# A graph network whose instruction order a planner writes: bias rows by an eight-column matmul, more raw weight buffers on two queues, and TensorE's clock in the planner's estimate

## The chip, the cores and the metric

One Trainium2 chip, one core of it. The metric is the device time of one execution in microseconds. The kernel before took 3004.77 us, the median of three runs (3003.74, 3004.77 and 3006.28).

## The reference

Thirty-two independent graphs of 512 nodes with 128 features go through four layers. Each layer takes a layer norm and a ReLU of x, runs its graph network on the result, and adds that to x.

```
# layer 0: maximum over neighbours
p = x @ (W1 - W2); q = x @ W2
out[i] = max over j of relu(p[i] + q[j] + b) * adj[i, j]

# layer 1: four steps, tanh, with earlier outputs stacked in front of later steps
src_agg = l2norm(adj, rows) @ (nodes @ ws + bs)
dst_agg = l2norm(adj, columns).T @ (nodes @ wd + bd)
self_rep = nodes @ wn + bn
out = tanh(concat(src_agg, self_rep, dst_agg) @ wu + bu)

# layer 2: mean over neighbours
out = (adj / rowsum) @ (x @ weight) + bias

# layer 3: four steps of a GRU
m = adj.T @ (h @ weight[i]); gx = m @ w_ih.T + b_ih; gh = h @ w_hh.T + b_hh
r = sigmoid(xr + hr); z = sigmoid(xz + hz); n = tanh(xn + r * hn)
h = (1 - z) * n + z * h
```

Everything is fp32. The adjacency matrix holds zeros and ones, about one in 32 of them ones.

## The kernel before

**One order for everything.** A batch is one graph. The Python functions `prepare`, `gathers`, `layer1` and `layer23` do not issue instructions. They note operations on a `Flow` object, each with its engine, an assumed duration, the operations it depends on and a due time. `Flow.run` then plays a little model of the five engines: `step` picks, among the operations whose inputs are ready and whose buffers are free, the one that can begin first (among equals the one that is due first), issues it, and moves the model's time on. The kernel's instructions stand on each engine in the order in which `step` issued them, and the engine works them off in that order. All of them are issued by one line in `step`, so that every row of the profile names line 496; tiles tell the operations apart.

**Due times and leads.** The due time of an operation is its part's place times `PACE`, less the assumed length of the work behind it in its part, less a lead. Each stage of a batch has its lead in `LEADS` (line 40). Place n is the batch's number, shifted for the last four by `LAST`. The weights are two parts ahead of the batches, `first` and `rest`, with the places in `WEIGHTS`. At most `AHEAD` = 6 parts are open at a time. Operations of some five batches are therefore mixed on each engine.

```python
PACE = 45.29
AHEAD = 6
WEIGHTS = (-4.52, -3.22)
```

**A batch.**
- `prepare`: norm of x; transposes of the adjacency matrix (tiles `pat`, then `at`); `pq`, the products with W; counts of neighbours as a matmul with a triangle of ones (`pc`, copied to `cc`, and by small DMAs on SP to `ccd`); keys of the neighbours that the counting leaves (`pkey`, whose eight largest DVE takes as `top`, and `idx` from it). `qn` goes to a table in DRAM, `qtab`.
- `gathers`: the first four neighbours in each group of rows by one-hot matrices `oh` that DVE makes and PE multiplies with `qhl` (`pa`), with a running maximum `acc` on DVE; up to seven further neighbours by 28 indirect DMAs on POOL from `qtab` (`gm`, `G`), with maxima on DVE. At the end `px`, `x1`, and four loads `an` of the adjacency matrix.
- `layer1`: `xn` is split into a high and a low part (`hi`, `lo`) so that two fp32r products with `at` and `an` (`pg`) give the aggregation in nearly fp32. The four steps multiply the results with folded weights `w1` in fp32 (`pu`), with the bias rows `b8` as a first product, with `rows`. After tanh the feature `f` is transposed again (`pf`) for the next step.
- `layer23`: layer 2 (`pg2`, `mT2`, `po`), then four GRU steps (`pk` for two gates, `pg3` for the messages, `mT`, `phn`, `pxn`). A step ends with a chain on two engines, from `pxn` over DVE, tanh on ACT and two more DVE operations to the new state, which PE transposes (`ph`) and ACT and DVE split into `hi` and `lo` for the next step. The output is stored by ACT's queue.

**Buffers.** PSUM has 8 banks, kept by `BANKS` = (2, 1, 2, 1) for four stages, with two more for whoever needs one. Scratch tiles are rings with one to six slots; weights borrow the rings that the batches use later.

**The weights.** `FastWeights.rest` (line 646) loads 16 bias rows and two blocks of GRU biases into `brow`, one DMA each on SP, and transposes them (`pb`, `bcol`). For each of the four steps of layer 1 it loads `wu` and, one after the other through one ring "f", `ws`, `wn` and `wd`; each is transposed (`pwt`), copied by DVE (`wt`), multiplied with `wu` (`pw`) and copied by ACT (`w1`). The two bias rows of a step are products with one column (`pv`); DVE splits them into a high and a low half (`both`), and eight one-row DMAs on SP for each step spread them over the eight rows of `b8`. Then come the weights of layers 2 and 3: `graw_hh` and `graw_ih` of the four GRU steps go through one ring, "gate1", all on SP, and are transposed (`pg_hh`, `pg_ih`).

Of the kernel before, what the change touches and what calls it, by code (L numbers as in the profile page):

```python
# [13 lines left out]
F32 = mybir.dt.float32  # L14
# [10 lines left out]
P = 128  # L25
# [6 lines left out]
KEY = float(ROWS)  # L32
CODES = ((0, 1), (P, 1), (2 * P, 2), (4 * P, 4))
NLEFT = 7
PACE = 45.29
SPACING = 1.8
AHEAD = 6
BANKS = (2, 1, 2, 1)

LEADS = {  # L40
    "prepare": -31.3, "counts": -26.1, "keys": -29.9, "rows": -0.7,
    "gather0": 21.0, "gather1": 4.8, "gather2": 6.6, "gather3": -2.6,
    "first": 14.3, "layer1": -15.8, "layer10": -31.7, "layer11": -34.7,
    "layer12": -17.6, "layer13": -49.5, "layer2": 17.3, "layer3": 7.8,
    "layer30": 58.6, "layer31": 78.0, "layer32": 33.2, "layer33": 37.4,
    "out": 22.6,
}
LAST = (0.0, 0.0, 0.06, -0.57, -0.08)
WEIGHTS = (-4.52, -3.22)
LN_EPS = 1e-5  # L50
L2_EPS = 1e-12
LOWEST = float(np.finfo(np.float32).min)
# [226 lines left out]
class Flow:  # L279
# [6 lines left out]

    LAT = 0.06
    LOAD = 0.25
    EVENT = 0.13
    ENGINES = ("pe", "vec", "act", "pool", "sync")  # L290

    def __init__(self, nc, pace, ahead, slack=0.0):
        self.nc, self.pace, self.ahead, self.slack = nc, pace, ahead, slack
        self.rings, self.part, self.lanes = {}, [], {}
        self.lead = 0.0
        self.free = dict.fromkeys(self.ENGINES, 0.0)
        self.busy = dict.fromkeys(self.ENGINES, 0.0)
        self.gathered, self.port, self.turn, self.queue = 0.0, 0.0, 0, {}
        self.seen = {e: {} for e in self.ENGINES}
        self.waiting = {e: [] for e in self.ENGINES}  # L300
        self.vec = Engine(self, "vec", nc.vector)
        self.act = Engine(self, "act", nc.scalar)
        self.pool = Engine(self, "pool", nc.gpsimd)
        self.sync = Engine(self, "sync", nc.sync)
# [22 lines left out]
    def cost(self, engine, op, outs, ins):  # L327

        aps = outs + ins
        n = max(a.free_size() for a in aps)  # L330
        o = outs[0].free_size()
        if "dma" in op:
            if engine != "pool":
                width = 2 if outs[0].dtype == BF16 else 4
                return 0.4, 2.0 + outs[0].size() * width / 1.5e5
            return (1.25, 6.0) if "indirect" in op else (0.7, 4.0)
        if engine == "vec":
            if op == "tensor_scalar" and o > 256:
                t = o / 1920.0 + 0.157
            elif op == "bn_stats":  # L340
                t = 0.28
            else:
                t = (o if op != "max" else n) / 960.0 + 0.15
                if op == "scalar_tensor_tensor" and len(ins) == 3:
                    t += 0.06
            return t - 0.082 + (0.08 if len(outs) > 1 else 0.0), 0.082
        if engine == "act":
            t = o / 1200.0 + 0.16 + 0.1 * (len(ins) - 1) + (0.04 if in_sbuf(ins[0]) else 0.0)
            return t - 0.1 + (0.2 if len(outs) > 1 else 0.0), 0.1
        if op == "tensor_tensor" and o < 64:  # L350
            return 1.1 if o < 8 else 1.7, 0.0
        two = op in ("tensor_tensor", "tensor_add", "tensor_sub", "tensor_mul")
        return (o / 408.0 + 0.05 if two and o > 64 else o / 1100.0 + 0.18), 0.0
# [99 lines left out]
    def step(self):  # L453
# [20 lines left out]
        seen.update(need)  # L474
        self.turn += 1
        op.turn = self.turn
        cost = op.cost + (self.EVENT * max(0, len(need) - 1) if op.engine != "pe" else 0.0)
        op.end = self.free[op.engine] = t + cost
        if op.port:
            self.port = op.end  # L480
# [23 lines left out]
                self.enter(u)  # L504
        self.log(op, t)
        return op

    def log(self, op, t):
        pass
# [55 lines left out]
class FastWeights:  # L565
# [5 lines left out]
    def __init__(self, nc, F, a, const, mid, ps):  # L571
# [37 lines left out]
        for t in range(n // P):  # L609
            nc.vector.tensor_scalar(  # L610
                self.code[:, t, :], ident, code[:, t : t + 1], None, ALU.mult
            )
        self.nc, self.a, self.const, self.n = nc, a, const, n

    def own(self, shape, dtype, name):
# [30 lines left out]
    def rest(self):  # L646
# [13 lines left out]
        col, at = {}, 0  # L660
        for key, src, m in rows:
            col[key] = at
            F.sync.dma_start(out=brow[at : at + m, :], in_=src)
            at += m
        pb = self.psum("pb")
        F.tr(pb[:, 0, :], brow, ident)
# [7 lines left out]


        self.w1, self.bu = [], self.own([P, NL1], F32, "bu")
        b8 = self.temp("hg", "b8")
        for i in range(NL1):
            ch = NCH[i]
            wu = self.temp("x2", f"wu{i}")[:, 0:3, :]  # L680
            F.sync.dma_start(out=wu, in_=a[f"L1_gnn_wu{i}"].rearrange("(c p) v -> p c v", p=P))
            w1 = self.own([P, 3, ch, P], F32, f"w1_{i}")
            for k, nm in enumerate(("ws", "wn", "wd")):
                w = self.temp("f", f"{nm}{i}")[:, 0:ch, :]
                F.sync.dma_start(
                    out=w, in_=a[f"L1_gnn_{nm}{i}"].rearrange("(c p) v -> p c v", p=P)
                )
                pt = self.psum(f"pwt_{i}_{k}")
                for c in range(ch):
                    F.tr(pt[:, c, :], w[:, c, :], ident)  # L690
                wt = self.temp("gate0", f"wt_{i}_{k}")[:, 0:ch, :]
                F.vec.tensor_copy(wt, pt[:, 0:ch, :])
                pw = self.psum(f"pw_{i}_{k}")
                for c in range(ch):
                    F.mm(pw[:, c, :], wt[:, c, :], wu[:, k, :], start=True, stop=True)
                F.act.copy(w1[:, k, :, :], pw[:, 0:ch, :])
            self.w1.append(w1)
            pv = self.psum(f"pv_{i}")
            c = col["bn", i]
            F.mm(pv[:, 2, 0:1], wu[:, 1, :], bcol[:, c : c + 1], start=True, stop=True)  # L700
            for k, nm in enumerate(("bs", "bd")):
                c = col[nm, i]
                F.mm(pv[0:1, k, :], bcol[:, c : c + 1], wu[:, 2 * k, :], start=True, stop=True)
            c = col["bu", i]
            F.vec.tensor_add(self.bu[:, i : i + 1], bcol[:, c : c + 1], pv[:, 2, 0:1])
            both = self.temp("agf1", f"both_{i}", True)
            part = both[0:1, 0, 0:256].bitcast(F32R)
            F.vec.tensor_copy(part, pv[0:1, 0:2, :].rearrange("p k d -> p (k d)"))
            F.vec.tensor_sub(
                both[0:1, 1, 0:256], pv[0:1, 0:2, :].rearrange("p k d -> p (k d)"),  # L710
                both[0:1, 0, 0:256],
            )
            for h in range(2):
                for g in range(2):
                    for k in range(2):
                        r = 4 * h + 2 * g + k
                        F.sync.dma_start(
                            out=b8[r : r + 1, i, :], in_=both[0:1, h, k * P : (k + 1) * P]
                        )
        self.b8 = self.own([8, NL1, P], F32R, "b8r")  # L720
        F.vec.tensor_copy(self.b8, b8[0:8, :, :])

        self.w2 = self.own([P, P], F32, "w2")
        F.sync.dma_start(out=self.w2, in_=a["L2_gnn_weight"])
        self.b2 = self.own([P, P], F32, "b2")
# [10 lines left out]
        self.gh, self.gm = [], []  # L736
        for l in range(NL3):
            for nm, dst in (("hh", self.gh), ("ih", self.gm)):
                g = self.temp("gate1", f"graw_{nm}{l}")[:, 0:3, :]
                F.sync.dma_start(  # L740
                    out=g, in_=a[f"L3_gnn_w_{nm}"][l].rearrange("(g p) c -> p g c", p=P)
                )
                pg = self.psum(f"pg_{nm}{l}")
                for k in range(3):
                    F.tr(pg[:, k, :], g[:, k, :], ident)
                t = self.own([P, 3, P], F32, f"g_{nm}{l}")
                if nm == "hh":
                    F.vec.tensor_copy(t, pg[:, 0:3, :])
                else:
                    gt = self.temp("xn2", f"gt_{l}")[:, 0:3, :]  # L750
                    F.vec.tensor_copy(gt, pg[:, 0:3, :])
                    pf = self.psum(f"pf_{l}")
                    F.mm(
                        pf[:, 0:3, :].rearrange("p t d -> p (t d)"), w3t[:, l, :],
                        gt.rearrange("p t d -> p (t d)"), start=True, stop=True,
                    )
                    F.act.copy(t, pf[:, 0:3, :])
                dst.append(t)
# [12 lines left out]
def fast(ctx: ExitStack, tc: tile.TileContext, a: dict, out: bass.AP, bad):  # L771
# [9 lines left out]
    dram = ctx.enter_context(tc.tile_pool(name="table", bufs=1, space=DRAM))  # L781

    F = Flow(nc, PACE, AHEAD)
    F.share(ps, 8, {f"ps{s}": n for s, n in enumerate(BANKS)})

    def bank(s, shape, dtype, name):
        return F.tile(ps, shape, dtype, f"ps{s}", name, BANKS[s])
# [388 lines left out]
    def batch(b):  # L1176
# [8 lines left out]

    places = [b - LAST[max(0, b - B + len(LAST) - 1)] for b in range(B)]
    F.run(
        [(WEIGHTS[0], W.first), (WEIGHTS[1], W.rest)]
        + [(p, partial(batch, b)) for b, p in enumerate(places)]
    )  # L1190

# [469 lines left out]
```

## Time and profile before

| what | value |
|---|---|
| median of three runs | 3004.77 us (3003.74 to 3006.28) |
| profiled execution | 3005.68 us, span 3004.0 us |
| PE busy | 2821.0 us, 94% of the span |
| DVE busy | 2403.8 us, 80% |
| POOL busy | 1798.9 us, 60% |
| ACT busy | 1214.9 us, 40% |
| granted TensorE clock | 0.979 of full speed, mean |
| chain that ended last | PE 77%, DVE 12%, issue 4%, ACT 2%, DMA 1%, POOL 1% |

The profile is one execution. PE is TensorE's products, PEld its weight loads, DVE VectorE, ACT ScalarE, POOL GpSimd, SP SyncE; a q behind a name is that engine's DMA queue. The row of slices gives busy tenths in 40 equal slices of the span, 75.1 us each, and PEclk the clock that TensorE was granted, in tenths. An f32 matmul stands as two records. A list of waits gives, for each engine and tile, for whom it waited: us in total, times, longest. The chain that ended last follows the work back from the last instruction. In what follows "the list" of an engine is the order of its instructions in the built program.

### The profile page before, as it was taken

Reading aid. Unit: us, or ns where it says so; the run is one execution under the profiler, and the core shown is the slowest. Engines: PE = TensorE matmul, PEld = TensorE weight load, DVE = VectorE, ACT = ScalarE, POOL = GpSimd, SP = SyncE. Lnnn points to the kernel's source line nnn. Section 1 sums busy time; section 2 is a strip of 40 time slices with the busy share of each in tenths; the row PEclk is TensorE's granted clock in tenths of the full one; section 3 lists DMA queues with packets and bytes.
Section 4 is the critical chain, followed back from the end, with each engine's and each line's share of the span. In section 5 each row is a group of like instructions: output and inputs, shape, how many; then the busy total and the mean of one; then the engine's idle time right before and its main releaser. Section 6 shows DMA issues by size and latency. Waiting matters only on the chain.

```text
span 3004.0 us, 37228 instructions
## 1 busy us (share of the span) xinstructions
PE 2821.0 (94%) x11233; PEld 1741.0 (58%) x11233; DVE 2403.8 (80%) x5364; ACT 1214.9 (40%) x2516; POOL 1798.9 (60%) x2000
## 2 busy tenths in 40 slices
PE   4688989999999999999999999999999999999985
PEld 3455656666666666666666666666666666655542
DVE  5887879888888988888888888888988888886422
ACT  2333434444444434444444434444434444432322
POOL 3666666666666666666666666666666666655211
PEclk7899999999999999999999999999999999999997
DMA  5533343433344334333433433344333334333000
GB/s 142 122 80 67 77 84 74 82 69 67 71 85 85 81 73 84 60 64 86 85 83 73 85 61 71 76 84 85 75 80 79 66 64 85 67 57 58 11 4 5
DMA packets 192289, 218.42 MB, mean 73 GB/s; under 512 B 31401, under 2 KB 140625, under 8 KB 192081
## 3 DMA queue, kind: packets, MB, share of 16 engines
q0 software_dynamic: 47104, 92.34, 22.2%
q1 hardware_dynamic: 77392, 64.90, 7.2%
q10 hardware_dynamic: 67584, 58.73, 6.3%
q8 instruction: 91, 1.49, 0.2%
q14 instruction: 118, 0.96, 0.1%
HBM read 164.32 MB, written 17.96 MB: 61 GB/s over the span
## 4 chain that ended last, share of the span: by engine, by line
PE 77%; DVE 12%; issue 4%; ACT 2%; DMA 1%; POOL 1%; ACTq 0%; SPq 0%; DVEq 0%; POOLq 0%
PE pg L496 23%; PE pu L496 18%; PE pk L496 15%; PE pa L496 6%; PE phn L496 4%; PE pxn L496 4%; DVE acc L496 3%; PE pkey L496 2%; PE pf L496 2%; PE ph L496 1%; DVE qhl L496 1%; DVE nn L496 1%; DVE x L496 1%; PE pc L496 1%; PE pt L496 1%
## 5 line engine op out<-in xcount | busy, mean ns | idle before, releaser
L496 POOL DMA_INDIRECT G<-qtab,idx x768 | 824.6, 1074 | 602.6 <-DVE gm L496 487.9
L496 DVE TENSOR_TENSOR acc<-acc,pa 128x512 f32<-128x512 f32 x992 | 674.2, 680 | 146.7 <-PE pa L496 134.0
L496 PE MATMUL pa<-oh,qhl 128*128 128x512 f32 x1024 | 472.6, 515 | 12.5 <-DVE oh L496 6.7
L496 PE MATMUL pg<-an,hi 128*128 128x512 f32 x1024 | 461.3, 451 | 1.1 <-ACT hi L496 0.7
L496 PE MATMUL pu<-ag,w 128*128 128x512 f32 x896 | 449.9, 596 | 1.1 <-DVE ag L496 1.1
L496 PE MATMUL pg<-an,lo 128*128 128x512 f32 x1024 | 435.2, 426 | 0.7 <-POOL lo L496 0.7
L496 DVE TENSOR_SCALAR oh<-ccd 128x1024 fp32r<-128x1024 bf16 x512 | 401.2, 802 | 10.3 <-PE pa L496 10.3
L496 PE MATMUL pg<-at,hi 128*128 128x512 f32 x640 | 289.1, 452 | 13.9 <-ACT hi L496 9.2
L496 PE MATMUL pg<-at,lo 128*128 128x512 f32 x640 | 297.0, 465 | 3.4 <-POOL lo L496 2.8
L496 PEld LDWEIGHTS pa<-oh,qhl 128*128 128x128 f32 x1024 | 197.2, 194 | 147.0 <-issue 52.5
L496 PE MATMUL pk<-h,g_hh 128*128 128x512 f32 x512 | 262.7, 618 | 4.4 <-DVE acc L496 1.9
L496 DVE TENSOR_TENSOR gm<-gm,G 128x128 f32<-128x128 f32 x768 | 260.8, 340 | 3.9 <-DMA G<-qtab,idx 3.1
L496 ACT ACTIVATE xn<-x,shift,rstd 128x128 f32<-128x128 f32 x512 | 212.4, 484 | 110.1 <-POOL shift L496 109.4
L496 PEld LDWEIGHTS pg<-an,hi 128*128 128x128 f32 x1024 | 194.0, 189 | 95.5 <-issue 50.7
L496 PEld LDWEIGHTS pg<-an,lo 128*128 128x128 f32 x1024 | 193.9, 189 | 87.0 <-issue 40.9
L496 PE MATMUL pk<-mT,g_ih 128*128 128x512 f32 x512 | 240.8, 593 | 2.2 <-ACT mT L496 2.2
L496 ACT COPY mT<-pg 128x512 f32<-128x512 f32 x160 | 93.7, 585 | 354.6 <-PE pg L496 354.0
L496 PEld LDWEIGHTS pu<-ag,w 128*128 128x128 f32 x896 | 166.9, 190 | 114.5 <-issue 82.2
L496 ACT ACTIVATE gate<-pk,bsum 128x512 f32<-128x512 f32 x256 | 175.4, 686 | 139.2 <-PE pk L496 132.2
L496 POOL TENSOR_TENSOR rstd<-rstd,mhalf 128x4 f32<-128x4 f32 x128 | 145.9, 1140 | 139.4 <-DVE shift L496 138.6
L496 ACT CAST hi<-ph 128x512 fp32r<-128x512 f32 x96 | 56.2, 586 | 382.2 <-PE ph L496 382.2
L496 DVE TENSOR_TENSOR ag<-pg,rbc 128x512 f32<-128x512 f32 x256 | 174.5, 682 | 21.3 <-PE pg L496 18.2
(161 smaller groups left out, 5043.3 us busy)
## 6 DMA issues: line engine op xcount, KB each, us to landing
af<-in_adj_dram ACTq DMA_DIRECT2D x32, 1024.0 KB
ccd<-cc SPq DMA_DIRECT2D x512, 64.0 KB
an<-in_adj_dram POOLq DMA_DIRECT2D x128, 256.0 KB, 4.3
x<-in_x_dram ACTq DMA_DIRECT2D x64, 256.0 KB
rbc<-scal SPq DMA_DIRECT2D x32, 512.0 KB
G<-qtab,idx POOLq DMA_INDIRECT x768, 3.8
qtab<-qn SPq DMA_DIRECT2D x128, 64.0 KB
out_dram<-xo ACTq DMA_DIRECT2D x32, 256.0 KB
```

The costliest lines, as they stand in the source:

```text
L496: op.fn(*(real(v) for v in op.args), **{k: real(v) for k, v in op.kw.items()})
```

## The change

- **Bias rows of layer 1.** The rows are products with an eight-column matrix `bm`, zero but for four columns that hold bs (or bd), so that `pv` has eight rows at once. ACT copies the high half (`hi`), DVE forms the low half with the column signs in `sign` and writes `b8` itself. The 32 one-row DMAs go.
- **Raw buffers and queues.** `ws`, `wn` and `wd` have the rings "f", "hg" and "hT1"; `wt` alternates between two; `graw_hh` and `graw_ih` have a ring each. Every second of `brow`, the loads of `wn` and those of `graw_ih` are issued by ACT in place of SP.
- **A third part of weights.** The weights of layers 2 and 3 and the mask are a part of their own, `last`.
- **The planner.** Its model lets PE operations take twice as long while the modelled clock is low (`clock`, a window of 3.413 us, with 0.42 and 0.84 as the busy shares at which it changes). It assumes other issue times and rates of DMAs. `spin` is None throughout. `LEADS`, `LAST`, `WEIGHTS`, `PACE` and `AHEAD` have new values.

```diff
-PACE = 45.29
+PACE = 45.28
-AHEAD = 6
+AHEAD = 5
 LEADS = {
-    "prepare": -31.3, "counts": -26.1, "keys": -29.9, "rows": -0.7,
-    "gather0": 21.0, "gather1": 4.8, "gather2": 6.6, "gather3": -2.6,
-    "first": 14.3, "layer1": -15.8, "layer10": -31.7, "layer11": -34.7,
-    "layer12": -17.6, "layer13": -49.5, "layer2": 17.3, "layer3": 7.8,
-    "layer30": 58.6, "layer31": 78.0, "layer32": 33.2, "layer33": 37.4,
-    "out": 22.6,
+    "prepare": -10.5, "counts": -26.1, "keys": -17.2, "rows": 12.1,
+    "gather0": 33.8, "gather1": 17.1, "gather2": 28.7, "gather3": 20.8,
+    "first": 38.4, "layer1": 7.7, "layer10": -8.2, "layer11": -16.0,
+    "layer12": -4.3, "layer13": -36.8, "layer2": 30.0, "layer3": 15.0,
+    "layer30": 46.7, "layer31": 87.3, "layer32": 33.3, "layer33": 25.4,
+    "out": 34.2,
 }
-LAST = (0.0, 0.0, 0.06, -0.57, -0.08)
-WEIGHTS = (-4.52, -3.22)
+LAST = (0.0, 0.16, 0.23, -0.28, 1.01)
+WEIGHTS = (-4.94, -3.26, -2.97)
...
+        self.spin, self.window, self.active, self.rate = None, 0, 0.0, 1.0
...
-                return 0.4, 2.0 + outs[0].size() * width / 1.5e5
+                return 0.48 if engine == "sync" else 0.42, 2.0 + outs[0].size() * width / 1.2e5
...
+        if op.engine == "pe":
+            t = self.clock(op, t)
         cost = op.cost + (self.EVENT * max(0, len(need) - 1) if op.engine != "pe" else 0.0)
+        if op.engine == "pe":
+            cost /= self.rate
+            self.active += cost
...
+    def clock(self, op, t):
+        gap = t - self.free["pe"]
+        n = int(0.7 * (gap - 0.4) / self.SPIN)
+        if self.spin and gap > self.IDLE and n > 0:
...
+        while t >= (self.window + 1) * self.WINDOW:
+            share = self.active / self.WINDOW
+            if share < 0.42:
+                self.rate = 0.5
+            elif share > 0.84:
+                self.rate = 1.0
+            self.window += 1
+            self.active = max(0.0, self.active - self.WINDOW)
+        return t
...
-            F.sync.dma_start(out=brow[at : at + m, :], in_=src)
+            (F.sync, F.act)[len(col) % 2].dma_start(out=brow[at : at + m, :], in_=src)
...
+        self.b8 = self.own([8, NL1, P], F32R, "b8r")
+        bm = self.own([P, NL1, 2, 8], F32, "bm")
+        F.pool.memset(bm, 0.0)
+        for i in range(NL1):
+            for k, nm in enumerate(("bs", "bd")):
+                c = col[nm, i]
+                F.act.copy(bm[:, i, k, k::2], bcol[:, c : c + 1].to_broadcast([P, 4]))
...
-                w = self.temp("f", f"{nm}{i}")[:, 0:ch, :]
-                F.sync.dma_start(
+                w = self.temp(("f", "hg", "hT1")[k], f"{nm}{i}")[:, 0:ch, :]
+                (F.sync, F.act)[k % 2].dma_start(
...
-            for k, nm in enumerate(("bs", "bd")):
-                c = col[nm, i]
-                F.mm(pv[0:1, k, :], bcol[:, c : c + 1], wu[:, 2 * k, :], start=True, stop=True)
+            for k in range(2):
+                F.mm(
+                    pv[0:8, 0, :], bm[:, i, k, :], wu[:, 2 * k, :],
+                    start=(k == 0), stop=(k == 1), group=pv,
+                )
...
-            for h in range(2):
-                for g in range(2):
-                    for k in range(2):
-                        r = 4 * h + 2 * g + k
-                        F.sync.dma_start(
-                            out=b8[r : r + 1, i, :], in_=both[0:1, h, k * P : (k + 1) * P]
-                        )
-        F.vec.tensor_copy(self.b8, b8[0:8, :, :])
+            hi = F.tile(self.mid, [P, 4, P], F32R, "hi1", f"bhi_{i}", 1)[0:8, 0, :]
+            F.act.copy(hi, pv[0:8, 0, :])
+            full = self.temp("nn", f"bfull_{i}")[0:8, 0, :]
+            F.vec.tensor_scalar(full, pv[0:8, 0, :], self.sign[0:8, 1:2], None, ALU.mult)
+            F.vec.scalar_tensor_tensor(
+                self.b8[:, i, :], hi.bitcast(F32), self.sign[0:8, 0:1], full, ALU.mult, ALU.add
+            )
+    def last(self):
...
-                g = self.temp("gate1", f"graw_{nm}{l}")[:, 0:3, :]
-                F.sync.dma_start(
+                q = nm == "ih"
+                g = self.temp(("gate1", "xn1")[q], f"graw_{nm}{l}")[:, 0:3, :]
+                (F.sync, F.act)[q].dma_start(
...
-    F.share(ps, 8, {f"ps{s}": n for s, n in enumerate(BANKS)})
+    F.share(ps, 8, {f"ps{s}": n for s, n in enumerate(BANKS)} | {"idle": 0})
...
-        [(WEIGHTS[0], W.first), (WEIGHTS[1], W.rest)]
+        list(zip(WEIGHTS, (W.first, W.rest, W.last)))
```

## The prediction

> **What bounds the kernel now.** The page first: TensorE is busy nearly the whole time, and the row of slices shows where it is not: the first five slices and the last three.
>
> ```profile
> PE 2821.0 (94%) x11233; PEld 1741.0 (58%) x11233; DVE 2403.8 (80%) x5364; ACT 1214.9 (40%) x2516; POOL 1798.9 (60%) x2000
> PE   4688989999999999999999999999999999999985
> PEclk7899999999999999999999999999999999999997
> ```
>
> Then busy times by stretch. Columns: start and end, length, then busy time of PE, PEld, DVE, ACT and POOL, then TensorE's granted clock, DMA share, GB/s.
>
> ```profile
> 50.00:75.00 25.00, 17.24 (x52) 10.53 (x52) 18.19 (x46) 1.38 (x4) 10.92 (x12) 0.52 0.57 121
> 100.00:150.00 50.00, 30.84 (x111) 19.32 (x112) 40.06 (x85) 15.61 (x41) 29.96 (x38) 0.80 0.58 131
> ...
> 350.00:437.00 87.00, 77.99 (x319) 48.30 (x318) 72.12 (x161) 34.98 (x76) 50.88 (x58) 0.98 0.36 69
> 437.00:524.00 87.00, 85.54 (x345) 53.04 (x344) 74.73 (x168) 36.58 (x76) 56.25 (x63) 1.00 0.36 73
> 2432.00:2519.00 87.00, 85.70 (x349) 53.35 (x348) 74.79 (x167) 37.65 (x80) 55.97 (x62) 1.00 0.38 77
> 2606.00:2693.00 87.00, 81.78 (x302) 48.92 (x301) 72.16 (x154) 30.36 (x60) 51.54 (x53) 1.00 0.32 58
> 2693.00:2780.00 87.00, 84.02 (x324) 50.52 (x323) 59.13 (x135) 30.93 (x57) 50.85 (x58) 1.00 0.36 58
> ```
>
> One batch takes 86.95 us in the middle (the chain shows "issue 1.92" at 1011.58, 1098.55 and 1185.53). There, as in 2432 to 2519, PE idles 87 - 85.70 = 1.3 us: TensorE is the bound, and only its own work or its rare waits count. Those waits are two, the same in every batch:
>
> ```profile
> PE ph L496 <- DVE h L496: 6.4, 11, 0.6
> PE po L496 <- DVE x L496: 6.2, 12, 0.5
> ```
>
> (us in total, times, longest; stretch 1000 to 2000.) The start is bound otherwise. In 20 to 150 PE waits for the raw weights:
>
> ```profile
> PE pg_hh L496 <- DMA graw_hh<-in_L_gnn_w_hh_dram: 9.5, 2, 5.1
> PE pwt L496 <- DMA wn<-in_L_gnn_wn_dram: 9.2, 3, 3.5
> PE pwt L496 <- DMA wd<-in_L_gnn_wd_dram: 5.9, 1, 5.9
> PE pwt L496 <- DMA ws<-in_L_gnn_ws_dram: 4.6, 3, 2.3
> ```
>
> With graw_ih (2.1) that is 31.3 us. Batch 0 waits with it, since the engines run their lists in order: its 28 row gathers, whose maxima stand on DVE between copies of weights, run from 35.4 to 114.7, and its layer 1 begins on PE at 136.5.
>
> **What the Trainium skill says.** "Perfetto Trace Analysis", Sequencer Loop: a sequencer reads the next instruction, and an engine instruction waits for its semaphore. The trace agrees: DVE stands 3.44 us before a g_hh copy at 124.76, with maxima of batch 1 behind it. "DMA: Bandwidth & Descriptors", Issuing engines are not separate DMA queues: a second issuing engine saves only the issue time. Here one b issue takes 0.58 us on SP (median of 32), so issue time is not small at this start. "TensorE: Matmul & The Clock Gate", What's actually happening: a mostly idle window of 3.4 us halves the clock. The trace agrees: 0.52 granted in 50 to 75, 1.00 in the middle.
>
> **The change part by part.**
>
> *Bias rows.* Gone: 32 one-row copies b<-both on SP, 32 x 0.58 = 18.6 us of its queue between 38 and 99, where ccd copies, wn and wd stand behind them; 8 DVE operations both (0.40 each) and the b8r cast, before which DVE stood 3.3 us at 103. New: 8 small ACT copies into bm (0.25 each by the 0.25 of sct, 2 us) and one POOL memset; 4 ACT copies hi and 8 DVE operations of 8 x 128 (0.28 by a 128 x 128 copy). PE: as many products, with 8 columns for 1. No row shows that width; the pv records took 0.15 to 0.25 each, so between nothing and 0.1 more for each of 16, at most 2 us: taken as 0. About even in engine time; a chain through DMA goes.
>
> *Raw buffers and two queues.* ws, wn, wd get a buffer each, graw_hh and graw_ih one each; 17 issues move from SP to ACT (9 brow, 4 wn, 4 graw_ih; SP's list goes from 848 DMAs to 799, with the 32). A transfer can now start before the transposes ahead of it. Of the 31.3 us some 20 should go. The first bias wait (pb, 13.4 us, which ends at 18.9) shrinks by 9 brow issues of 0.29, 2.6 us.
>
> *What is late next.* In the built order, DVE has three wt copies ahead of the last statistics of batch 0, so its rstd waits for wd (SP's 17th DMA); ACT has bm copies, three w copies and a bias copy ahead of batch 0's xn, and issues the 9 brow loads ahead of x. Before, xn came at 22.4 with one weight ahead. By the waits that now stand ahead (one transfer landing, 2 to 3 us, two transpose-copy-product rounds of about 1.5 us) batch 0 starts about 6 us later. Against that fewer waits stand among its gathers: 19 of them took 56.9 to 98.4, 2.3 us apart, where the first eight were 1.35 apart, an excess of 18 x 0.95 = 17 us, and another 8.7 passed to the next at 107.1 while DVE stood at b8r. If half of these 26 us goes, the start gains 13 - 6 = **7 us**. Bounds: -26 (all of it, no delay) to +8 (delay alone).
>
> *Clock in the estimate.* clock() touches the planner's own times only: spin stays None, so no filler product is issued and the ring "idle" is never given. It, LEADS, AHEAD and the new DMA costs act through the order alone, and this is the largest part. Same work: 9497 PE operations in both, 83.3 us a batch by intervals of the trace (128x512 fp32r 0.23, f32 0.86, transposes 0.11). But before, the list from one batch's first pc to the next's is the same from batch 6 on, up to 29. In the changed one it repeats only from batch 18 to 28; for 6 to 16 it has half to three quarters of its places (0.51 to 0.78) in common with the repeated one. **Twelve more irregular stretches** (6 to 17; 29 is one too, and is taken with the end).
>
> The price of one: before has four near them. PE's idle time above 1.3 is 7.7 in 350 to 437 (list 0.77 alike; 3.4 of it a wait for rows), 0.2 in 437 to 524 (0.94 alike), 3.9 in 2606 to 2693 (0.80) and 1.7 in the next. Mean 3.4; 12 x 3.4 = **+41 us**. Where it comes from: between pxn and the transposes ph of the new state stand the gate's DVE and ACT steps, and other PE work must cover them. A cover is the work, by these durations, that stands between in PE's list. Before, the regular list has 7.1, 4.8, 6.2 and 5.6 us there for the four GRU steps, and ph still waits 0.6 us at the last; at 2652.88 a cover of 5.3 gave a wait of 1.65. The changed list has 3.0 in batch 6, 3.7 and 2.6 in 8, 4.0 in 10, 3.7 in 11 and 13. Summed over batches 5 to 14, what is short of 5.6 comes to 20 us, and hi copies of layer 1 with 0.0 to 0.7 (batches 11 to 14), where 1.1 sufficed, add 3. DVE, 86% busy (74.8 of 87), adds queueing that PE's list doesn't show.
>
> AHEAD of 5 for 6 costs nothing by itself once the list repeats: in it a batch ends 366 us of PE work after its prep began, under the 416 of five batches; PACE moves by 0.01.
>
> *The regular list, 11 periods.* Covers again: tanh to pf of layer 1, 0.7 becomes 1.6; mT2 to po: 1.4 to 1.6; the last ph: 5.6 to 5.1; tanh to px: 1.7 to 0.9. Two waits shorter by about 0.25, two longer by up to 0.5: taken as 0, bounds -0.5 to +1 a batch (-6 to +11).
>
> *End.* The new LAST changes the interleaving of the last four; in both lists the last ph of batch 30 leaves 34 us of PE work to batch 31 alone, which took 90 us (2914 to 3004) in both engine waits and slow clock. Taken as 0, bounds -6 to +10.
>
> Sum on the profiled execution (3005.68; span 3004.0): 3005.7 - 7 + 41 + 0 + 0 = 3039.7. It lay 0.9 above the median of the runs (3004.77), so **3039 us**.
>
> **The rivals.**
> - *The irregular list costs much more* (chance 0.20). DVE's list is as irregular, and at 86% it has no time to catch up; each stretch costs what 350 to 437 cost. For: that window is the nearest in likeness. Against: 3.4 of its 7.7 was one wait for rows at the start. 12 x 6 = 72, start -4, from 3005: 3073.
> - *The start decides, and the kernel is faster* (0.16). Place: the 31.3 us that PE waits for raw weights up to 124, and batch 0's gathers behind them. If batch 0's layer 1 begins by 112 instead of 136.5, everything after it moves by 25; and if the irregular stretches cost 0.7 each, near the 0.2 of 437 to 524, they give back 8: 2988. It decides as soon as the start's gain exceeds twelve times the stretch's price, so at 25 below 2.1 us. Against: 6 and more us of new waits ahead of xn; three of the four windows at 1.7 or more.
> - *No difference* (0.08): the two cancel, 20 against 20; or the order is covered by slack and the weights were hidden behind gathers whose pace is POOL's (1.07 us each). 3004.
> - *The likeliest, as summed* (0.56), own range 3014 to 3060.
>
> **How the numbers follow.** A measurement of this kernel tells about 0.2%, 6 us, from no change. Faster is the second rival, 0.16; same the third, 0.08; slower the rest, 0.76. The range takes in most of the faster case and of the dearer one: 2988 to 3080.
>
> **What would show it.** Right: in the windows PE busy below 84 of 87 between about 600 and 1600 and 85.7 after about 1700; ph <- DVE h far above 6.4 us in 1000 us; batch 0's pg<-at near 128; no b<-both; the waits for wn, wd, ws and graw below 12 us together. Wrong: PE busy 985 of 1000 from 600 on, or a first pg<-at after 140.

## The result, and the profile after

The changed kernel takes 3086.71 us (median of four runs, 3082.33 to 3090.70) beside 3005.49 us for the kernel before (four runs): 2.7% slower, ratio 1.0271, 95% interval 1.0253 to 1.0289. The forecast was 3039 us with a range up to 3080: right in direction, with a loss of 34 us where 81 were measured. The profiled execution took 3082.33 us, span 3080.5.

The page of the changed kernel first: busy time, then the slices (77.0 us each).

```profile
PE 2856.1 (93%) x11233; PEld 1749.7 (57%) x11233; DVE 2359.7 (77%) x5363; ACT 1217.5 (40%) x2528; POOL 1840.3 (60%) x2005
PE   6789999999998999999999999999999999899985
PEclk8899999999999999999999999999999999999997
```

TensorE executes the same 11,233 records and yet is "busy" 35 us longer than before (2821.0). The start has filled up. In the middle the tenths hide everything: a slice at 93% and one at 98% both read 9. So busy times by stretch, columns as in the prediction (ends, length, then PE, PEld, DVE, ACT, POOL, granted clock, DMA share, GB/s):

```profile
50.00:75.00 25.00, 18.20 (x86) 13.23 (x87) 22.89 (x51) 6.98 (x18) 18.36 (x20) 0.80 0.78 159
100.00:150.00 50.00, 38.24 (x158) 22.98 (x158) 43.33 (x95) 20.01 (x46) 31.98 (x37) 0.83 0.42 81
569.00:1598.00 1029.00, 969.70 (x3821) 593.49 (x3820) 806.43 (x1835) 414.06 (x860) 644.75 (x692) 0.99 0.38 72
2432.00:2519.00 87.00, 85.05 (x346) 52.94 (x345) 73.11 (x166) 37.62 (x78) 56.49 (x63) 1.00 0.37 77
2606.00:2693.00 87.00, 76.66 (x292) 45.05 (x290) 69.18 (x161) 32.09 (x68) 51.62 (x55) 0.98 0.38 75
```

The third line reaches from layer 1 of batch 5 to layer 1 of batch 16. The same stretch of work in the kernel before, the same view:

```profile
588.00:1544.00 956.00, 942.33 (x3820) 586.67 (x3818) 821.76 (x1828) 413.82 (x859) 615.82 (x684) 1.00 0.38 77
```

3821 products against 3820: the same work takes 1029 us instead of 956, **73 us more in 11 periods, 6.6 each** (from batch 4 on it is 77 in 12, 6.4 each). PE's idle time grows from 13.7 to 59.3 us (+45.6), and its busy time for the same products from 942.3 to 969.7 (+27.4). Where it waits there (us in total, times, longest; the waits of PE in 569 to 1598 of the changed kernel):

```profile
PE pu L504 <- ACT rows L504: 10.8, 6, 3.7
PE ph L504 <- DVE h L504: 6.2, 8, 1.3
PE pg L504 <- ACT hi L504: 5.6, 6, 1.7
PE pa L504 <- DVE acc L504: 5.1, 8, 1.5
PE po L504 <- DVE x L504: 4.1, 7, 0.8
PE pg L504 <- DVE acc L504: 3.6, 3, 1.7
PE pk L504 <- DVE acc L504: 3.2, 2, 2.0
PE ph L504 <- DVE idx L504: 2.0, 1, 2.0
PE pa L504 <- DVE shift L504: 1.8, 2, 1.0
```

Before, two kinds made up the list. Now there are more than twenty, each a few times. That looks like no single resource, but readers that stand too near behind their writers in many places; it is a reading of the list, which the experiments test in part.

In 20 to 150 PE waited 31.3 us for raw weights before. Now the same view has two waits for DMA, the first of them new:

```profile
PE pw3t L504 <- DMA w<-in_L_gnn_weight_dram: 3.8, 1, 3.8
PE pg_hh L504 <- DMA graw_hh<-in_L_gnn_w_hh_dram: 2.1, 1, 2.1
```

To follow a delay through the kernel, take from the instruction records when a batch's layer 1 begins on PE (its first product `pu`), and compare the same batch in two kernels. All experiments below are shown in the same way; the last column is the difference of the spans (before: 3004.0).

| kernel, against before (us) | batch 0 | 5 | 16 | 27 | 31 | span |
|---|---|---|---|---|---|---|
| before, at | 144 | 588 | 1544 | 2500 | 2842 | 3004.0 |
| changed | -23 | -19 | +54 | +57 | +76 | +76.5 |
| e1_regular | -15 | -17 | -12 | -7 | +2 | -1.1 |
| e2_weights | +4 | +3 | +4 | +4 | +5 | +5.4 |
| e3_last | -22 | -19 | +61 | +65 | +69 | +69.7 |
| e4_irregular | +5 | +6 | +79 | +133 | +133 | +130.1 |
| e5_order | -3 | -10 | +80 | +161 | +172 | +169.5 |
| e6_narrow_after | -23 | -29 | +27 | +21 | +35 | +34.4 |
| e7_narrow_regular | -17 | -37 | -42 | -48 | -42 | -43.8 |
| e8_lead0 | -10 | -22 | -22 | -22 | -20 | -23.0 |
| e9_lead0_oldw | -11 | -12 | -12 | -13 | -11 | -13.3 |
| e10_best | -17 | -3 | -3 | -4 | -1 | +3.9 |
| e11_row8 | -22 | -19 | +47 | +50 | +69 | +70.2 |
| e12_row8_regular | -18 | -21 | -15 | -11 | -1 | +2.5 |

The changed kernel's row gives the terms of the prediction as measured: start -19, irregular stretches +73, regular list +3, end +19, together +76. Rows of one execution are good to some us (e3_last has the changed kernel's list up to batch 28, and stands 7 us beside it at batch 16).

### The profile page after: what moved, and what is told of

It reads as the page before. It is cut to its first block, busy times and chain, and to the rows that moved or that the text cites. A ratio compares the mean times of both kernels' runs of the same rounds, so it can differ in the third digit from the quotient of the medians.

```text
span 3080.5 us, 37155 instructions
## 1 busy us (share of the span) xinstructions
PE 2856.1 (93%) x11233; PEld 1749.7 (57%) x11233; DVE 2359.7 (77%) x5363; ACT 1217.5 (40%) x2528; POOL 1840.3 (60%) x2005
## 4 chain that ended last, share of the span: by engine, by line
PE 68%; DVE 14%; POOL 5%; issue 5%; ACT 5%; DMA 3%; ACTq 1%; SPq 0%; DVEq 0%; POOLq 0%
PE pg L504 19%; PE pu L504 16%; PE pk L504 14%; PE pa L504 5%; PE phn L504 3%; PE pxn L504 3%; DVE acc L504 3%; POOL G L504 2%; DVE nn L504 2%; PE ph L504 2%; ACT xn L504 1%; DVE oh L504 1%; DVE x L504 1%; DVE st L504 1%; PE po L504 1%
## 5 line engine op out<-in xcount | busy, mean ns | idle before, releaser
L504 POOL DMA_INDIRECT G<-qtab,idx x768 | 843.1, 1098 | 583.0 <-DVE gm L504 436.6
L504 PE MATMUL pa<-oh,qhl 128*128 128x512 f32 x1024 | 480.4, 529 | 32.1 <-DVE acc L504 12.5
L504 DVE TENSOR_SCALAR oh<-ccd 128x1024 fp32r<-128x1024 bf16 x512 | 371.9, 737 | 10.1 <-PE pa L504 10.0
L504 DVE TENSOR_TENSOR gm<-gm,G 128x128 f32<-128x128 f32 x768 | 244.7, 322 | 15.5 <-DMA G<-qtab,idx 14.6
L504 DVE SCALAR_TENSOR_TENSOR nn<-phn,bcol,gate 128x512 f32<-128x512 f32 x128 | 95.7, 748 | 181.2 <-ACT gate L504 179.9
```

The costliest lines, as they stand in the source:

```text
L504: op.fn(*(real(v) for v in op.args), **{k: real(v) for k, v in op.kw.items()})
```

## The experiments

**Is it the irregular list?** e1_regular changes one literal. Its list of PE repeats from batch 6, and the repeated list is the one of the changed kernel.

```diff
-PACE = 45.28
+PACE = 45.27
```

> The changed kernel with one literal moved: PACE 45.27 for 45.28. Its TensorE list repeats from batch 6 on instead of from batch 18, and the repeated list is the same one. Theory (the irregular stretches cost 6.6 us each: batches 5 to 16 of the changed kernel fell 73 us behind in 11 periods): the stretches from 6 on run at about 87 us a batch, so about 3086 - 73 = 3013 us, between 3000 and 3025. The price of the prediction (3.4 each): 3086 - 37 = 3049. Rival, the loss is in the weights part, the new repeated list or DMA queues and not in the order's irregularity: 3075 to 3090.

Measured: 3003.64 us (ratio to before 0.9992, interval 0.9979 to 1.0006). From batch 5 to 16, and beside it the changed kernel's 1029 us above:

```profile
571.00:1532.00 961.00, 942.59 (x3817) 587.37 (x3817) 809.01 (x1826) 413.33 (x858) 630.00 (x684) 1.00 0.37 76
```

PE's busy time is back at 942.6, idle 18.4. All 83 us of the loss go (of the spans' 78, 65 by batch 16 and most of the rest after batch 27, where the list is another one too), with the weights part, the leads, the clock in the estimate, AHEAD, LAST and the queues in place. The order is the loss, most of it in the irregular stretches of the middle; the rival is out.

**The weights part alone, and the mirror of e1.** e2_weights takes the new weights part and undoes every setting of the order. e4_irregular is e2_weights with two other numbers in WEIGHTS.

```diff
# e2_weights against the changed kernel (LEADS and the DMA costs as before the change)
-PACE = 45.28
+PACE = 45.29
-AHEAD = 5
+AHEAD = 6
-LAST = (0.0, 0.16, 0.23, -0.28, 1.01)
-WEIGHTS = (-4.94, -3.26, -2.97)
+LAST = (0.0, 0.0, 0.06, -0.57, -0.08)
+WEIGHTS = (-4.94, -3.26, -2.6)
-            t = self.clock(op, t)
+            pass
# e4_irregular against e2_weights
-WEIGHTS = (-4.94, -3.26, -2.6)
+WEIGHTS = (-4.94, -3.22, -2.97)
```

> The weights part of the changed kernel (bias rows of eight columns, more raw buffers, two queues, the third function last) with PACE, AHEAD, LEADS, LAST and DMA costs of the kernel before and without the clock in the estimate; WEIGHTS (-4.94, -3.26, -2.6). Its TensorE list repeats from batch 7 on, the same repeated list as before the change. Theory: the start alone gains some 20 us (layer 1 of batch 0 came 23 us earlier in the changed kernel), one more irregular stretch costs up to 7: 2985 us, between 2975 and 2998, faster than before. Rival, the weights part delays batches 1 to 5 as much as it helps batch 0: 3000 to 3010.

> As e2_weights, with WEIGHTS (-4.94, -3.22, -2.97) for (-4.94, -3.26, -2.6), that is, with one function of the weights 1.8 us of PACE later in the planner's places and the last one sooner. The work and all other settings are the same; its list never falls into the repeated one of e2_weights, so 23 more stretches are irregular (7 to 29). Theory at 6.6 us each: 152 us above e2_weights, about 3137. The prediction's 3.4 each: 78 above, about 3063. Rival, irregularity by itself costs nothing and the new LEADS or the clock made a poor order: within 15 us of e2_weights.

Measured: e2_weights 3010.20 us (1.0020, 1.0011 to 1.0028), e4_irregular 3134.14 us (1.0432, 1.0404 to 1.0461). Two findings. First, my theory of the start fell: with the order as before, the new weights part gains nothing: the row gathers of batch 0 begin at 62.8 us for 35.4, its layer 1 comes 4 us later, and everything keeps that lag. Second, the same work in another order costs 124 us more.

The expectation of e4_irregular counted its stretches wrongly, which makes the run more telling. Its list does fall into the repeated one: it is alike in 10 and 11 and from 27 on (0.94 in 9 and 26), so that 7, 8 and 12 to 25 are irregular beside e2_weights, 16 and not 23, at 124 / 16 = 7.8 us each. The step from layer 1 of one batch to layer 1 of the next nearly coincides with the stretch two numbers higher (878 to 965 us for batches 8 and 9, the stretch of batch 10 from 892 to 979), and there the records show it: layer 1 of the batches 8, 9 and 10 begins 87 us apart, and so it does from 24 to 28. Nearly all the delay falls into the stretches between, up to 16 us in one (layer 1 of batch 11 to 12). Where the list repeats, nothing is lost; where it doesn't, a stretch costs from next to nothing (0.8 us, 20 to 21) to 16.

**The end.** e3_last gives the changed kernel its old LAST back; the list is the same up to batch 28.

```diff
-LAST = (0.0, 0.16, 0.23, -0.28, 1.01)
+LAST = (0.0, 0.0, 0.06, -0.57, -0.08)
```

> The changed kernel with LAST of the kernel before (0.0, 0.0, 0.06, -0.57, -0.08). The list is the same up to batch 28, and batch 29 now repeats too. Theory: most of the 19 us lost after batch 27 come from the new placing of the last batches: 3086 - 15 = 3071, between 3064 and 3077. Rival, the end pays for the new repeated list whatever LAST says: 3082 to 3090.

Measured: 3069.10 us (1.0211, 1.0186 to 1.0236), 17.6 below the changed kernel, near the theory. From layer 1 of batch 27 to the end, in the order changed kernel, before, e3_last:

```profile
2557.00:3080.50 523.50, 454.50 (x1613) 265.19 (x1612) 294.03 (x665) 174.78 (x338) 216.53 (x235) 0.94 0.20 39
```

```profile
2500.00:3004.00 504.00, 446.85 (x1610) 262.59 (x1609) 293.83 (x652) 170.94 (x327) 211.77 (x230) 0.95 0.20 37
```

```profile
2565.00:3073.70 508.70, 451.50 (x1612) 266.57 (x1612) 295.95 (x665) 174.67 (x338) 217.47 (x235) 0.94 0.20 40
```

Idle time 69.0, 57.2 and 57.2 us: the old LAST brings PE's idle time at the end back to what it was. The loss sits already between batches 27 and 28 (96 us for 87) and again from 29 on, not in the last batch alone. But the new LAST is not dear in itself: e1_regular has it too, and from batch 27 to the end it loses 6 us where the changed kernel loses 19. What LAST costs depends on the order that it meets.

**Whose start is it?** e5_order is the reverse of e2_weights: the old weights part, with the new PACE, AHEAD, LEADS, LAST, DMA costs and clock.

> The kernel before with its own weights part (bias rows by DMA, one queue, two functions) and only the order settings of the changed kernel: PACE 45.28, AHEAD 5, LEADS, LAST, the DMA costs and the clock in the estimate. What is read is the start: layer 1 of batch 0 on TensorE began at 144 us before and at 121 in the changed kernel; with the new weights part alone (e2_weights) it began at 148. Theory now, the new LEADS and the clock put batch 0 ahead of the weights: 118 to 130 here. Rival, both are needed, because the old weights part holds the engines' lists up whatever the order: 140 or later. Its list never repeats from one batch to the next, about 24 more irregular stretches than before, so with 6 us each the end is near 3004 - 20 + 144 + 15 = 3143; with 3.4 each near 3081.

Measured: 3180.93 us (1.0586, 1.0555 to 1.0617; two runs). Batch 0 begins layer 1 at 141, so for that batch the rival holds: both parts are needed. But batches 2 to 4 come 17 to 18 us early, in the changed kernel 16 to 23, so for them the order settings bring much of the gain without the new weights. By batch 5 it is 10 of 19. Then 25 stretches that never repeat cost 179 us to batch 30 (-10 to +169), 7.2 each; at the 6 of the expectation the end would have been near 3143.

**Is it DVE's load?** In e6_narrow_after and e7_narrow_regular the 992 maxima of acc take 64 columns instead of 512; the order on every engine stays that of the changed kernel and of e1_regular. What acc holds is not computed in full.

```diff
                         F.vec.tensor_max(acc, acc, flat(pa))
+                        F.part[-1].narrow = True
...
+        if getattr(op, "narrow", False):
+            op.args = tuple(v[:, 0:64] for v in op.args)
         op.fn(*(real(v) for v in op.args), **{k: real(v) for k, v in op.kw.items()})
```

> The changed kernel with the same list on every engine; 992 maxima acc<-acc,pa on DVE take 64 of their 512 columns, so part of the computation of acc is left out. It frees about 992 x 0.5 = 496 us of DVE (77% busy to about 61%). Read against e7_narrow_regular, which has the same cut. Theory A, an irregular list costs because DVE, 86% busy in the middle, queues: with DVE at 65% the difference to the regular list falls from 83 us to under 20, so about 3000. Theory B, it costs because TensorE's list puts a reader too soon after its writer's chain over ACT, POOL and a DMA, whatever DVE's load: the difference stays above 50, and this run takes about 3055 to 3075.

> e1_regular (PACE 45.27, list repeating from batch 6) with the same cut of the acc maxima as e6_narrow_after. TensorE is the bound in the repeated stretches (idle 1 to 2 us of 87), so little can be gained there; the start and the end, where DVE is waited for, gain some: 2985 to 3000 under both theories. It is the measure for e6_narrow_after.

Measured: 3039.19 us (1.0115, 1.0092 to 1.0137) and 2964.22 us (0.9868, 0.9852 to 0.9885). Both fell further than expected, but the difference between irregular and regular list went only from 83 to 75 us. From batch 5 to 16, e6_narrow_after, then e7_narrow_regular:

```profile
560.00:1571.00 1011.00, 962.89 (x3820) 593.36 (x3819) 668.49 (x1835) 414.19 (x860) 647.96 (x691) 0.99 0.39 73
```

```profile
551.00:1502.00 951.00, 938.16 (x3818) 587.59 (x3818) 669.77 (x1827) 413.23 (x859) 640.23 (x685) 1.00 0.37 77
```

DVE is busy 66% instead of 78% of the irregular stretch, and the same work is still 60 us apart (68 with full maxima, 1029 against 961). DVE's average load is worth some 8 of 68; theory A is out. That leaves theory B, the chains' latency at the place where the list reads them, for the rest; this is argued by exclusion, and only one chain is tested below. Which engine's place in the list is wrong in each case wasn't taken apart.

**One wait taken away.** The longest kind was rows. Its DMA stands on SP, and SP waits (the queue's waits in 1190 to 1217 of the changed kernel, us in total, times, longest) for transposes that read the buffer it shares with f:

```profile
SPq L504 <- PE px L504: 17.2, 1, 17.2
```

Once issued at 1208.4, it still needed some 8 us to land (ACT's rows begins at 1216.6); ACT had issued loads of af and x from 1206.7 on, and the DMA share was 0.99 in 1208 to 1217. e11_row8 and e12_row8_regular give row8 a buffer of its own, with the order unchanged (the same two lines stand in both kinds of rings).

```diff
+        if name.startswith("row8_"):
+            return self.pool.tile(shape, dtype, tag="row8", name=name, bufs=1)
```

> The changed kernel with the same order on every engine; the tile row8 has a buffer of its own instead of one shared with f, so that its DMA on SP no longer waits for the transposes px that read f. In the changed kernel PE's waits for rows, which come through this DMA, are the largest kind between 600 and 1600: 10.8 us in 6 waits, the longest 3.7. Theory, a long wait costs its idle time and then again some in a TensorE clock at half speed right after it (30.6 us at half clock in that stretch, none before the change): 10.8 + about 7 = 18 us less, 3060 to 3075. Rival, the next reader is late for another reason and waits instead: 3080 or more.

> e1_regular (list repeating from batch 6) with a buffer of its own for row8, the measure for e11_row8. In its repeated list rows are waited for once a batch, 0.6 us each (6.5 in 1000 us), no clock loss. If these go: 22 x 0.6 = 13 us less, about 2990. If the work behind them waits for something else then, 3000 to 3005.

Measured: 3076.28 us (1.0235, 1.0217 to 1.0253), 10.4 below the changed kernel, and 3003.00 us (0.9998, 0.9990 to 1.0005), nothing. Waits of PE from batch 5 to 16 in e11_row8:

```profile
PE pg L508 <- ACT hi L508: 7.8, 9, 1.7
PE ph L508 <- DVE h L508: 6.9, 9, 1.3
...
PE pg L508 <- POOL lo L508: 2.1, 4, 0.6
```

The waits for rows fall from 10.8 to 0.6 us, those for hi, h and lo grow by 2.2, 0.7 and 1.0, and the stretch gets 8 us shorter, not 18. The theory overstated it: part of a removed wait goes to the next reader, and half speed stays, 27.3 us at other places for 30.7, though the longest wait is gone. In e12_row8_regular rows are still waited for 6.7 us, 11 times; there the shared buffer isn't what they wait for.

**A version that keeps the start.** e8_lead0 takes the new LEADS for batch 0 alone, the new weights part and DMA costs, and else the order of before.

```diff
+LATER = {
+    "prepare": -31.3, "counts": -26.1, "keys": -29.9, "rows": -0.7,
...
+}
+def leads(b):
+    return LEADS if b < 1 else LATER
...
-        F.lead = LEADS["rows"]
+        F.lead = leads(b)["rows"]
```

> The changed kernel's weights part and its LEADS for batch 0 only; from batch 1 on LEADS of the kernel before, with its PACE 45.29, AHEAD 6 and LAST; the new DMA costs, no clock. Its list repeats from batch 7 and the repeated list is that of before (86.95 us a batch). Theory: the start of the changed kernel (some 15 to 20 us), no irregular stretch more than one, the old end: 2983 to 2995, the first version faster than before by more than 0.2%. Rival, the start's gain is given back by batches 1 to 5 when the old LEADS take over, as in e2_weights: 3003 to 3012.

Measured: **2981.99 us, ratio to before 0.9921, interval 0.9899 to 0.9943**: 0.8% faster than the kernel before. Its page, the lines of the same kind as above:

```profile
PE 2816.3 (94%) x11233; PEld 1739.9 (58%) x11233; DVE 2387.8 (80%) x5363; ACT 1215.9 (41%) x2528; POOL 1806.3 (61%) x2005
PE   5799999999999999999999999999999999999985
PEclk9799999999999999999999999999999999999997
```

The third slice is full, and all 22 us that batch 5 is early last to the end. e9_lead0_oldw is the same on the old weights part, with WEIGHTS (-4.52, -3.22); e10_best is e9_lead0_oldw with WEIGHTS (-4.52, -2.6).

> e8_lead0 without the new weights part: the kernel before (old bias rows, one queue, WEIGHTS (-4.52, -3.22)), with LEADS of the changed kernel for batch 0 alone and the new DMA costs. Its list repeats from batch 7 with the repeated list of before. It tells what of the start's gain (e8_lead0: batch 4 is 21 us early) comes from the weights part and what from the order of batch 0. Theory, from e5_order where batch 4 came 17 us early with the old weights: nearly all from the order, 2982 to 2992. Rival, the raw weights must get out of the way of batch 0 first: 2998 or more.

> As e9_lead0_oldw with WEIGHTS (-4.52, -2.6), so that the second weights function stands 28 us later in the planner's places; its list repeats from batch 4 instead of 7. Theory, three stretches fewer that are irregular, 6 us each at most: 2970 to 2985, the fastest so far. Rival, the weights now come late for layer 1 of batch 0 and batch 0 pays what the others gain: 2990 or more.

Measured: 2996.93 us (0.9977, 0.9968 to 0.9986) and 3003.05 us (0.9994, 0.9987 to 1.0002). e9_lead0_oldw lies between its theory and its rival. In the profiled executions 12 of the 22 us at batch 5 come with the old weights too; but that of e9_lead0_oldw (2992.54 us) was its fastest of twelve, and by the medians, each against the runs of the kernel before beside it, it is 7 of 21. So half or more of the gain needs the new part (in its new places), which with the old order (e2_weights) costs 4: it pays only if batch 0 is let ahead of it. e10_best went to its rival: layer 1 of batch 1 comes 8 us late, and of the 17 us that batch 0 was early, 3 are left by batch 5.

## Why the prediction was right in sign and wrong in size

**The price of an irregular stretch, the step that failed.** The count was right (they lie between batches 5 and 16, and e1_regular shows that they are the loss); the price of 3.4 us was not: 73 / 11 = 6.6. The prediction read it as PE's idle time above the regular 1.3 in windows of fixed length. In that currency it was not far off: 45.6 / 11 = 4.1, and its four samples were more alike the regular list (0.77 to 0.94) than the stretches to be priced (0.51 to 0.78). What it left out is the other 27.4 us, by which PE's busy time for the same products grew; it had counted the same work in both lists, 83.3 us a batch, and so put this at nothing. Up to 15.4 of them are TensorE's clock: by the clock records it stood at half speed for 30.7 us between 714.7 and 1516.9, in seven places, and never in that stretch before or in e1_regular. Two of them, with what stood ahead:

```profile
998.00:1001.40 3.40, 1.41 (x6) 0.87 (x7) 3.40 (x7) 0.21 (x1) 0.71 (x1) 1.00 0.01 2
1213.50:1216.50 3.00, 0.06 (x1) 0.00 (x0) 2.38 (x5) 0.00 (x0) 1.64 (x3) 1.00 1.09 339
1216.50:1223.30 6.80, 5.99 (x9) 2.80 (x9) 1.02 (x3) 2.78 (x6) 4.99 (x5) 0.50 0.63 110
```

PE waits 3.7 us for rows, to 1217.3, and from 1216.5 on the clock stands at 0.50 for 6.8 us: the wait costs some 3 us more. At 998 a wait of 2.0 us (the ph <- DVE idx of the list above) is enough; 3.4 us at half speed follow.

The 15.4 are arithmetic (30.7 x 0.5), not an experiment. Of the other 12 us a part may be the ends of products: around 1210 us products of 0.39 us begin 0.23 apart, so the last one before a wait stands 0.16 longer, and PE's busy time falls into 97 pieces without a gap here for 43 before; 54 x 0.16 is some 9 us, an estimate.

The prediction gave the clock no term in the middle, though its own line 350 to 437 has 0.98 (half speed from 412.4 to 415.8). The Trainium skill, "TensorE: Matmul & The Clock Gate", What's actually happening, has half speed follow at least one idle window of about 3.4 us; here windows with PE busy up to 1.58 of 3.40 us were enough, so the measurement goes beyond the page. Nor is every longer wait paid twice: of the nine over 1.5 us six stand just ahead of half speed, and three (1.9 us at 847, 1.7 at 936 and at 1086) don't.

**The place of the waits.** The prediction put the shortfall at ph <- h, "far above 6.4 us in 1000". It stayed at 6.2 in 1029; the waits came at rows, hi, acc and others. So covers at one kind of place were no measure of the sum. The rival "the irregular list costs much more" had the size (6 each) and the sign, and its reason, DVE at 86%, explains only 8 of 68 by e6 and e7.

**The start, -7.** Measured -19 at batch 5. The first pg<-at stood at 119.6, not near 128. The delay at batch 0 was there, but smaller than 6: xn begins 2 us later (24.4), the products `pq` and the first gather 4 later (30.9 for 26.6, 39.3 for 35.4); that half of the 26 us would go was too low. And its reason was too narrow: with the old weights e5_order is 10 us early at batch 5 and e9_lead0_oldw 12 (its median time is 7 us down), so the order settings bring a good part of it, and e8_lead0 shows that the weights part brings the rest only together with them. The waits for wn, wd, ws and graw came to 3.3 us (1.2 of it before 20 us), below the 12 named.

**The end, 0.** Measured +19. With the old LAST it is 5 in the trace of e3_last; the medians differ by 17.6. The step that failed looked at the work left to batch 31 alone, which takes 89 us for 90; the loss began with batch 27.

**Right:** the regular list (11 periods 959 us for 956, +3 within -6 to +11); bias rows about even (pv with eight columns 373 ns, with one 339, sixteen times); no b<-both; PE busy 941 of the 1000 us from 600 and 786 of the 800 from 1700.

**The sum.** -19 + 73 + 3 + 19 = +76 in place of -7 + 41 + 0 + 0 = +34. Of the 42 us between them the price is +32, the end +19, the regular list +3, and the start -12.

## What to carry to other kernels

Price a changed order by the time that the same work takes (pick two landmarks and count the products between them), not by idle time in fixed windows: more than a third of the loss showed as longer busy time here. Where instruction order comes from a greedy planner, a number changed by 0.01 can move the time by 83 us; build the order and look whether it settles before judging any other part of the change. A part that is meant to help the start pays only if the order lets the start use it; a setting that helps one batch can be given to that batch alone.

## What the runs showed of the hardware

The half clock didn't need a wait of a whole window. In these records the clock changes in steps of 3.413 us. Cut 569 to 1598 of the changed kernel at the places of the steps: the six steps at full speed in which PE was busy least (0.14 to 0.46 of the step) were all followed by half speed. Every other one had 0.54 or more, and only one of these, at 1510.0, was followed by it:

```profile
1510.00:1513.40 3.40, 2.17 (x8) 1.08 (x8) 2.36 (x4) 1.59 (x3) 2.92 (x4) 1.00 0.99 159
1513.40:1516.90 3.50, 3.50 (x7) 2.11 (x7) 1.40 (x3) 0.00 (x0) 2.65 (x3) 0.51 0.78 56
```

So the place of a wait among the steps counts, not its length alone. The 2.0 us that ph waits at 998.5 lie within one step (998.0 to 1001.4, PE busy 1.41 of 3.40, above), and half speed follows. In e11_row8, with the same list, the same wait of 2.0 us begins at 997.2 and is shared by two steps, and the clock stays at full speed. The border is not sharp: in e11_row8 a step with PE busy 0.47 was not followed by half speed, one with 0.50 was.

```profile
995.10:998.50 3.40, 1.91 (x21) 1.33 (x18) 3.40 (x6) 1.31 (x3) 0.91 (x1) 1.00 0.05 11
998.50:1001.90 3.40, 2.70 (x10) 1.53 (x11) 3.40 (x7) 0.58 (x1) 2.02 (x2) 1.00 0.12 16
```
